# Graph network of four layers on one core: in the second sweep, PSUM results leave by the scalar engine, row-tile pairs stand closer, score vectors are spread later, and the last row tile is treated like the others

## The chip, the cores and the metric

The kernel runs on one core of a Trainium2 chip. The metric is the device time of one execution in microseconds. The time before the change is 2900.31 us, the median of four runs that lie between 2897.81 and 2901.46. All data are 32-bit floats.

## The reference

Four graph layers follow one another on `x` (2708 x 512) with one dense adjacency matrix `adj` (2708 x 2708). Each is added to its input and normalized by rows. Cut to what matters:

```python
deg = jnp.maximum((adj != 0).astype(jnp.float32).sum(-1), 1.0)
x = _layernorm(x + _L0_gnn_ref(x, adj))           # adjacency with normalized mask, divided by its row sums
x = _layernorm(x + _L1_gnn_ref(x, adj, adj, ...)) # below
x = _layernorm(x + _L2_gnn_ref(x, adj, weight))   # x@w0 + adj@x@w1 + adj@adj@x@w2 + ...
x = _layernorm(x + _L3_gnn_ref(x, adj, deg, W, b))# relu((dinv*(adj+I)*dinv @ x + x) @ W + b)

def _L1_gnn_ref(x, adj_a, adj_b, W_sa, a_sa, W_gcnb, b_gcnb, Wa, ba, Wb, bb):
    attn_a = sigmoid(concatenate([adj_a @ x, x], 1) @ Wa.T + ba)
    attn_b = sigmoid(concatenate([adj_b @ x, x], 1) @ Wb.T + bb)
    h = x @ W_sa
    scores = (h @ a_sa[0, :Hd])[:, None] + (h @ a_sa[0, Hd:])[None, :]
    e = where(adj_a != 0, exp(-leaky_relu(scores, 0.01)), 0.0)
    x_a = (e / (e.sum(1, keepdims=True) + 1e-05)) @ h
    x_b = adj_b @ (x @ W_gcnb) + b_gcnb
    return sigmoid(attn_a * x_a + attn_b * x_b)
```

## The kernel before

**Sweeps.** The product of the adjacency matrix with a feature matrix is the kernel's work. It is done in seven sweeps over the matrix, and the sweep with index `s` starts at position `S[s] = 28 * s` of a list. A sweep uses a scheme of seven block products in place of eight: the matrix is cut into two by two blocks, VectorE makes sums of blocks of the adjacency (L405), and TensorE multiplies them (L460) with sums of blocks of the features, `B11`, `B21`, `B22`, `T1` to `T4`, whose tiles carry a letter from A to D for the step of 128 rows that they belong to. In the first two sweeps the rows of the result are cut into ranges, `RANGES = [(0, 384), (384, 384), (768, 256), (1024, 330)]` (start, width). Each range takes seven positions of the list; a product goes through ten steps `k`, two matmuls in each, that add up in the PSUM banks `accu`, `accc`, `accd` and `acca`.

**Order.** Every piece of work is put into a list with `at(position, function)`. The list is sorted by position, and the functions then issue their instructions in that order. Each engine runs its own instructions strictly in the order in which they were issued, and waits at the first one that is not ready. So a position in the list decides what stands behind what on every engine. Tiles come from pools with fixed numbers of buffers: a ring of 38 for adjacency tiles, 6 natural-layout tiles (`nat`), and the 8 banks of PSUM. The tile framework adds the semaphores.

**What the second sweep does.** It forms `adj @ x` for the second layer, with `x` the result of the first layer, whose last rows are still being normalized when the sweep starts (L818, then L557 to L569; the bank that L818 reads comes from L591). While the sweep runs, VectorE also counts the nonzero elements of each adjacency tile into `deg` (L966); SyncE loads those tiles (L396), and GpSimd stores their sums to `As` (L408) for later sweeps.

**Pairs of row tiles.** When a range's product is ready, `done1` multiplies it by `W_gcnb`. Two row tiles, one of each half of the rows, are done together with the same scheme of seven products, in `seven`. One bank holds the quarters `u` and `c`, another `d` and `a`, each 256 wide. Part 0 makes three products of two matmuls into `u`, `c` and `d`; part 1 makes four, which go on in `a`, `u`, `c` and `d`. After each part VectorE adds the quarters to the two output tiles `y` (L654), with the bias row `vec` in place of the old value where an output is touched for the first time. After part 1, ScalarE multiplies each tile of `y` by its gate (L1017), and GpSimd stores it to `XB` (L151). The pairs of one range run beside the next range's sweep. They are three, three and two, and the last range has none. The same `seven` serves the last sweep, where a list `scales` is given and line L656 is used in place of L654.

**Score vectors.** `spread_v` spreads four vectors of 512 numbers, held as columns in `vmat`, over all 128 partitions: sixteen transposes (L891) into four `pv` banks, and eight copies by ScalarE (L894) into tiles that the scheme has free. The function `score` multiplies row tiles by them on VectorE (L903). A row transposition into `ps_r` (L924) follows where the scores of a set of tiles are done.

**The last row tile.** At the end of the kernel the six last row tiles of the output are multiplied by the weights one by one. For the first five, function `b` makes a full-width product by `dense` (L608), one VectorE operation that scales and adds the bias (L1547), then `finish` with ReLU and sum (L1483), the layer norm with its last step on ScalarE (L567), and the store. For the sixth (83 rows) `b_last` does it in halves of 256 columns and divides the last step between ScalarE and VectorE.

Of the kernel before, what the change touches and what calls it, by code (L numbers as in the profile page):

```python
# [21 lines left out]
F32 = mybir.dt.float32  # L22
BF = mybir.dt.bfloat16
AF = mybir.ActivationFunctionType
ALU = mybir.AluOpType
P = 128
EPS = 1e-5
NH = 1354
# [40 lines left out]
def gnn_kernel(ctx: ExitStack, tc: tile.TileContext, x, adjT, w_sa, a_sa, w_gcn, b_gcn, wab, bab, w_hop, w_out,  # L69
               b_out, out):  # L70
    nc = tc.nc
    N, D = x.shape
    NT = 2 * KT
    DC = D // P
    HD = D // 2
# [5 lines left out]
    small = ctx.enter_context(tc.tile_pool(name="small", bufs=6))  # L81
# [9 lines left out]
    neg_half = const.tile([P, 1], F32, name="neg_half")  # L91
# [18 lines left out]
    rdeg_f = const.tile([P, 24], F32, name="rdeg_f")  # L110
# [36 lines left out]
    def move(queue, dst, src):  # L147

        m = dst.shape[0]
        c = m - m % 16 if m > 16 else m  # L150
        queue.dma_start(out=dst[:c], in_=src[:c])  # L151
        if c < m:
            queue.dma_start(out=dst[c:m], in_=src[c:m])
# [7 lines left out]
    def trans(nm):  # L161
        return pool.tile([P, 384], F32, name=nm, tag="ring", bufs=RING)
# [7 lines left out]
    def bank(nm, shape=None):  # L170
        return psum.tile(shape or [P, D], F32, name=nm, tag="x", bufs=8)
# [6 lines left out]
    def at(pos, fn, hold=False):  # L178

        def go():  # L180
            n = len(nc.cur_bb.bb.instructions)
            fn()
            held.update(range(n, len(nc.cur_bb.bb.instructions)))

        events.append((pos, len(events), go if hold else fn))
# [454 lines left out]
    def seven(part, Y, wop, H, lo, w, outs, scales, bases):  # L640

        if part == 0:
            x, y = bank("ps_7"), bank("ps_7")
            H.update(u=x[:, :HD], c=x[:, HD:], d=y[:, :HD], a=y[:, HD:])
        for home, a, v in SEV[part]:
            for c in range(2):
                nc.tensor.matmul(H[home][:w], Y[a, c][:, lo : lo + w], wop(v, c),  # L647
                                 start=part == 0 and home in "ud" and c == 0, stop=c == 1, skip_group_check=True)

        def acc(i, e, home, first=False):  # L650
            o = outs[i][:w, e * HD : (e + 1) * HD]
            b = bases[i][:w, e * HD : (e + 1) * HD] if first else o
            if scales is None:
                nc.vector.tensor_tensor(o, H[home][:w], b, ALU.add)  # L654
            else:
                nc.vector.scalar_tensor_tensor(o, H[home][:w], scales[i], b, ALU.mult, ALU.add)  # L656

        if part == 0:
            acc(0, 0, "u", True)
            acc(1, 1, "c", True)  # L660
            acc(1, 1, "d")
        else:
            acc(0, 0, "a")
            for i, e in ((1, 1), (0, 1), (1, 0)):
                acc(i, e, "u", (i, e) != (1, 1))
            acc(1, 0, "c")
            acc(0, 1, "d")

    def fetch(src, nm="ld"):
        t = nat(nm)  # L670
        move(nc.sync, t[: src.shape[0]], src)
        return t
# [4 lines left out]
    S = [28.0 * s for s in range(8)]  # L677
# [172 lines left out]
    for k in range(KW):  # L850
        f = k / KT
# [13 lines left out]
    W = {}  # L865
    vec = {}
# [26 lines left out]
                V[j, e] = homes[2 * j + e]  # L893
                nc.scalar.copy(V[j, e], ps[:, e * HD : (e + 1) * HD])  # L894

    at(S[1] + 0.5, spread_v)

    def score(t, w, got):
        x1 = got[t]
# [41 lines left out]
    i = 0  # L941
# [55 lines left out]
    def done1(p0, dp, last, R0, n, h, C, tiles):  # L997
        Z = {}

        def gates():  # L1000

            pg = bank("pg")
            for c in range(DC):
                nc.tensor.matmul(pg[32 * c : 32 * c + 32, :n], wab_pad[:, c, :], C[h, c][:, :n], start=True, stop=True)
            Z[0] = trans("zg")
            nc.scalar.copy(Z[0][:, :n], pg[:, :n])

        def gate_tile(i, t, lo, w):
            if i == 0:
                Z[1] = bank("pz", [P, 8])  # L1010
            pz = Z[1][:, 2 * i : 2 * i + 2]
            nc.tensor.matmul(pz[:w], Z[0][:, lo : lo + w], pick, start=i == 0, stop=True, skip_group_check=True)
            nc.vector.tensor_tensor(gate[:w, t, :], pz[:w], gate_x[:w, t, :], ALU.add)
            nc.scalar.activation(gate[:w, t, :], gate[:w, t, :], AF.Sigmoid)

        def finish(t, w, y):
            nc.scalar.mul(y[:w], y[:w], gate[:w, t, 1:2])  # L1017
            move(nc.gpsimd, XB[t], y[:w])

        at(p0 + 0.05, gates)  # L1020
        for i, (t, lo, w) in enumerate(tiles):
            def b(i=i, t=t, lo=lo, w=w):
                gate_tile(i, t, lo, w)
                if not last:
                    return
                px = dense(lambda c: C[h, c][:, lo : lo + w], W[1], w)
                y = nat("y")
                nc.vector.tensor_tensor(y[:w], px[:w], vec[1][:w], ALU.add)
                finish(t, w, y)

            at(p0 + 0.25 + (dp * i if last else 0.02 * i), b)
        if last or h:
            return

        Y = {}
        at(p0 + 0.3, lambda: Y.update(row_sums({(i, c): C[1 - i, c] for i in range(2) for c in range(DC)}, n)))
        for i, (t, lo, w) in enumerate(tiles):
            H, y = {}, []

            def b7(part, t=t, lo=lo, w=w, H=H, y=y):  # L1040
                if part == 0:
                    y.extend(nat("y") for _ in range(2))
                seven(part, Y, W[8], H, lo, w, y, None, [vec[1], vec[1]])
                if part == 1:
                    for j in range(2):
                        finish(t + KT * (1 - j), w, y[j])

            at(p0 + 0.6 + 1.1 * i, lambda f=b7: f(0))
            at(p0 + 0.6 + 1.1 * i + 0.2, lambda f=b7: f(1))

    sweep(S[1], RANGES, extra=extra1, done=done1, late=0.85, save=True)

# [425 lines left out]
    def done6(p0, dp, g, i0, n, h, cc, tiles):  # L1478
# [12 lines left out]
        for i, (s, lo, w) in enumerate(tiles[:3] if not end else ()):  # L1491
            H, got, z = {}, {}, []
            r = 12 * g + 6 * h + lo // P
# [14 lines left out]
            p = p0 + 0.35 + 0.95 * i  # L1508
# [3 lines left out]
        for i, (s, lo, w) in enumerate(tiles[3:] + tiles[:3] if end else ()):  # L1512
            got = {}
            r0 = i0 + s * n + lo

            def a(r0=r0, w=w, got=got):
                got["x"] = fetch2(X3, h, r0, w)

            def b_last(s=s, lo=lo, w=w, r0=r0, got=got):

                r = 12 * g + 6 * h + 3 * s + lo // P
                y = got["x"]
                st = small.tile([P, 2, 6], F32, name="st2", bufs=1)
                for e in range(2):
                    q = slice(e * HD, (e + 1) * HD)
                    px = bank("ps_d")
                    for c in range(DC):
                        nc.tensor.matmul(px[:w, q], cc(s, c)[:, lo : lo + w], W[6][c][:, q], start=c == 0,
                                         stop=c == DC - 1, skip_group_check=True)
                    nc.vector.scalar_tensor_tensor(px[:w, q], px[:w, q], rdeg_f[:w, r : r + 1], vec[6][:w, q], ALU.mult,  # L1530
                                                   ALU.add)
                    nc.vector.scalar_tensor_tensor(y[:w, q], px[:w, q], 0.0, y[:w, q], ALU.max, ALU.add)
                    nc.vector.bn_stats(st[:w, e, :], y[:w, q])
                mv = small.tile([P, 2], F32, name="mv")
                nc.vector.bn_aggr(mv[:w], st[:w])
                rstd = small.tile([P, 2], F32, name="rstd")
                nc.vector.tensor_scalar(rstd[:w, 0:1], mv[:w, 1:2], EPS, None, ALU.add)
                nc.gpsimd.tensor_tensor(rstd[:w, 1:2], rstd[:w, 0:1], neg_half[:w], ALU.pow)
                nc.vector.scalar_tensor_tensor(rstd[:w, 0:1], mv[:w, 0:1], -1.0, rstd[:w, 1:2], ALU.mult, ALU.mult)
                nc.scalar.activation(y[:w, :HD], y[:w, :HD], AF.Identity, bias=rstd[:w, 0:1], scale=rstd[:w, 1:2])  # L1540
                nc.vector.tensor_scalar(y[:w, HD:], y[:w, HD:], mv[:w, 0:1], rstd[:w, 1:2], ALU.subtract, ALU.mult)
                move(nc.sync, out[h * NH + r0 : h * NH + r0 + w, :], y[:w])

            def b(s=s, lo=lo, w=w, r0=r0, got=got):
                px = dense(lambda c: cc(s, c)[:, lo : lo + w], W[6], w)
                r = 12 * g + 6 * h + 3 * s + lo // P
                nc.vector.scalar_tensor_tensor(px[:w], px[:w], rdeg_f[:w, r : r + 1], vec[6][:w], ALU.mult, ALU.add)  # L1547
                finish(s, lo, w, got["x"], px)

            p = p0 - 0.095 + 0.14 * i  # L1550
            at(p - 0.6, a)
            at(p, b if i < 5 else b_last)

    sweep2(S[6], 0, done6, True)

# [8 lines left out]
    for n, i in enumerate(list(nc.cur_bb.bb.instructions)):  # L1564
        p = last if n < 3 * strict else done if n in held else {}
# [44 lines left out]
```

## Time and profile before

| | |
|---|---|
| median of four runs | 2900.31 us (2897.81 to 2901.46) |
| profiled execution, its own time | 2900.08 us |
| span of the profiled execution | 2898.3 us |
| outside the span | 1.78 us |
| mean granted TensorE clock | 0.995 |
| TensorE (PE) busy | 2841.8 us, 98% |
| VectorE (DVE) busy | 2270.5 us, 78% |
| ScalarE (ACT) busy | 563.7 us, 19% |
| GpSimd (POOL) busy | 618.5 us, 21% |

The profile is of one execution. Its engines are PE (TensorE's matmuls), PEld (its weight loads), DVE, ACT, POOL and SP (SyncE); SPq and ACTq stand for those engines' DMA issues. L12 is line 12 of the kernel. A row of the timeline gives the start in microseconds, the duration, the engine, the line, the operation, the tiles written and read, the shapes, and how many instructions are drawn together (x4); in brackets stands how long the engine was idle before it, and what ended that wait. Where instructions of one engine overlap, the distance of their starts is what each costs in a row. One matmul of 32-bit floats appears as two records.

### The profile page before, as it was taken

The page shows a single profiled execution, that of the slowest core. Times are in us where ns is not written, and L with a number is a line of the kernel's source. Part 1 is how long each engine was busy: PE and PEld are TensorE (multiplying, and loading weights), DVE is VectorE, ACT ScalarE, POOL GpSimd, SP SyncE. Part 2 cuts the span into 40 slices and gives each one's busy share as a digit, 9 for nine tenths or more (in the row PEclk, how much of TensorE's full clock was granted, in tenths as well). Part 3 has the DMA queues.
Part 4 walks back from the last instruction along what each step waited for, and adds up shares of the span by engine and source line. Part 5 has one row for each costly group of instructions (what it writes and reads, how often), then busy time and mean ns, then how long its engine had stood idle before and what let it go on. Part 6 is the DMA issues. An engine that isn't in the chain of part 4 may idle for free. (4 is left out here: it accounts for less than half of the span.)

```text
span 2898.3 us, 37726 instructions
## 1 busy us (share of the span) xinstructions
PE 2841.8 (98%) x10963; PEld 1874.5 (65%) x10963; DVE 2270.5 (78%) x5879; ACT 563.7 (19%) x1106; POOL 618.5 (21%) x1119
## 2 busy tenths in 40 slices
PE   7999999999999999999999999999999999999998
PEld 6655665567765666866666666666666666666665
DVE  6989698666647775776699787887878878799987
ACT  4544200101136544552100000000000100100001
POOL 0223223223320111122203123031230211501202
PEclk9999999999999999999999999999999999999999
DMA  7666466444544433565667767566675666754552
GB/s 231 211 192 188 139 199 219 128 155 137 175 148 118 135 119 96 145 197 157 201 195 231 221 186 249 166 199 212 186 249 167 183 196 182 233 163 143 174 142 91
DMA packets 373456, 511.52 MB, mean 176 GB/s; under 512 B 63723, under 2 KB 326629, under 8 KB 373249
## 3 DMA queue, kind: packets, MB, share of 16 engines
q1 hardware_dynamic: 307128, 372.01, 44.4%
q0 software_dynamic: 49536, 126.39, 12.7%
q10 hardware_dynamic: 16584, 10.71, 1.4%
q8 instruction: 87, 1.43, 0.2%
q14 instruction: 121, 0.98, 0.1%
HBM read 425.22 MB, written 83.67 MB: 176 GB/s over the span
## 5 line engine op out<-in xcount | busy, mean ns | idle before, releaser
L1223 DVE TENSOR_TENSOR z<-z 128x339 f32<-128x339 f32 (+1 forms) x966 | 454.0, 502 | 13.2 <-PE accu L1276 3.3
L1294 ACT COPY q<-accu 128x338 f32<-128x338 f32 (+1 forms) x84 | 34.6, 443 | 1005.1 <-PE accu L1276 976.6
L562 POOL TENSOR_TENSOR rstd<-rstd,neg_half 128x1 f32<-128x1 f32 (+3 forms) x91 | 58.4, 642 | 769.6 <-DVE rstd L561 518.8
L1276 PE MATMUL accc<-s,t 128*128 128x338 f32 (+1 forms) x644 | 198.2, 450 | 0.0
L1276 PE MATMUL accu<-z,t 128*128 128x338 f32 (+1 forms) x644 | 194.5, 449 | 2.3 <-DVE z L1223 2.3
L1276 PE MATMUL accc<-z,t 128*128 128x338 f32 (+1 forms) x644 | 194.8, 450 | 0.5 <-ACT q L1294 0.5
L1276 PE MATMUL accd<-z,t 128*128 128x338 f32 (+1 forms) x644 | 193.9, 448 | 0.6 <-DVE q L1358 0.6
L1409 POOL DMA_DIRECT2D Y<-y x192 | 104.8, 552 | 361.8 <-DVE y L1404 332.9
L405 DVE TENSOR_TENSOR a<-a,a 128x384 f32<-128x384 f32 (+2 forms) x330 | 161.8, 510 | 13.2 <-PE accu L460 12.0
L1276 PEld LDWEIGHTS accc<-z,t 128*128 128x128 f32 x644 | 122.9, 191 | 62.3 <-issue 1.8
L1276 PEld LDWEIGHTS accc<-s,t 128*128 128x128 f32 x644 | 121.0, 190 | 64.0 <-issue 7.5
L1276 PEld LDWEIGHTS accu<-z,t 128*128 128x128 f32 x644 | 121.8, 190 | 62.4 <-DVE z L1223 2.9
L1276 PEld LDWEIGHTS accd<-z,t 128*128 128x128 f32 x644 | 122.0, 190 | 60.4 <-DVE q L1358 1.5
L1223 DVE TENSOR_TENSOR s<-z 128x338 f32<-128x338 f32 (+1 forms) x322 | 149.5, 503 | 11.8 <-PE accc L1276 7.4
L1300 DVE TENSOR_TENSOR q<-q,accd 128x338 f32<-128x338 f32 (+1 forms) x112 | 55.9, 499 | 114.4 <-PE accd L1276 114.4
L1075 ACT ACTIVATE e<-row,neg_s 128x384 f32<-128x384 f32 (+5 forms) x176 | 100.4, 570 | 77.1 <-DVE e L1077 22.8
L1076 ACT ACTIVATE f<-row,neg_s 128x384 f32<-128x384 f32 (+5 forms) x176 | 99.9, 568 | 19.7 <-PE accc L460 6.3
L1077 DVE TENSOR_TENSOR e<-e,f 128x384 f32<-128x384 f32 (+5 forms) x176 | 87.1, 506 | 18.3 <-ACT f L1076 17.4
L966 DVE SCALAR_TENSOR_TENSOR deg<-a,deg 128x384 f32<-128x384 f32 (+2 forms) x152 | 74.9, 504 | 29.3 <-DMA a<-in_adjT 28.1
L408 POOL DMA_DIRECT2D As<-a x120 | 64.8, 543 | 92.9 <-DVE a L405 84.9
L1078 DVE SCALAR_TENSOR_TENSOR a<-a,e 128x384 f32<-128x384 f32 (+2 forms) x160 | 79.9, 507 | 5.0 <-DMA a<-in_adjT 3.1
L763 DVE SCALAR_TENSOR_TENSOR s<-a,row 128x384 f32<-128x384 f32 (+2 forms) x152 | 75.1, 506 | 6.0 <-ACT row L748 6.0
(689 smaller groups left out, 5963.0 us busy)
## 6 DMA issues: line engine op xcount, KB each, us to landing
z<-As SPq DMA_DIRECT2D x320, 169.5 KB
z<-As SPq DMA_DIRECT2D x320, 169.0 KB
a<-in_adjT SPq DMA_DIRECT2D x240, 192.0 KB
z<-in_adjT SPq DMA_DIRECT2D x240, 169.5 KB
z<-in_adjT SPq DMA_DIRECT2D x240, 169.0 KB
a<-in_adjT SPq DMA_DIRECT2D x120, 165.0 KB
a<-in_adjT SPq DMA_DIRECT2D x112, 128.0 KB
As<-a POOLq DMA_DIRECT2D x60, 192.0 KB, 3.9
```

The lines of the kernel that those rows point to most:

```text
L405: nc.vector.tensor_tensor(A[r, dst, k][:, :n], A[r, a, k][:, :n], A[r, b, k][:, :n], op)
L408: nc.gpsimd.dma_start(out=SD[m][k * P : (k + 1) * P, R0 : R0 + n], in_=A[r, dst, k][:, :n])
L562: nc.gpsimd.tensor_tensor(rstd[:w, 1:2], rstd[:w, 0:1], neg_half[:w], ALU.pow)
L763: nc.vector.scalar_tensor_tensor(t[:w, :n], a[:w, :n], 0.0, row[R0, h][:w, :n], ALU.is_gt, ALU.mult)
L966: nc.vector.scalar_tensor_tensor(d[:w, :n], a[:w, :n], 0.0, d[:w, :n], ALU.not_equal, ALU.add)
L1075: nc.scalar.activation(e[:w, :n], row[R0, h][0][:w, :n], AF.Exp, bias=neg_s[:w, t : t + 1])
L1076: nc.scalar.activation(f[:w, :n], row[R0, h][1][:w, :n], AF.Exp, bias=neg_s01[:w, t : t + 1])
L1077: nc.vector.tensor_tensor(e[:w, :n], e[:w, :n], f[:w, :n], ALU.min)
L1078: nc.vector.scalar_tensor_tensor(a[:w, :n], a[:w, :n], 0.0, e[:w, :n], ALU.not_equal, ALU.mult)
L1223: nc.vector.tensor_tensor(d[:, :n], Z[x + (k,)][:, :n], Z[y + (k,)][:, :n], op)
L1276: nc.tensor.matmul(B[home][:, :n], stat(v, k), a[:, :n], start=bool(start and k == 0), stop=k == nk - 1, skip_group_check=True)
L1409: nc.gpsimd.dma_start(out=rows[:, :, f * P : (f + 1) * P], in_=o[32 * f : 32 * (f + 1), : m * P].rearrange("p (b d) -> p b d", d=P))
```

## The change

It has four parts. In `seven`, where no `scales` are given (the second sweep), part 0 copies `u` and `c` out of PSUM by ScalarE; only `d` is added by VectorE, and the bias is added from SBUF by two more VectorE operations at the end of part 1. The pairs stand 0.56 of a position apart in place of 1.1, and the second part of each 0.26 after the first in place of 0.2. `spread_v` moves from 0.5 to 0.85 behind the start of the second sweep. `b_last` is gone, and the sixth of the last row tiles goes through `b`.

```diff
@@ seven
-        if part == 0:
+        if part == 0 and scales is None:
+
+            nc.scalar.copy(outs[0][:w, :HD], H["u"][:w])
+            nc.scalar.copy(outs[1][:w, HD:], H["c"][:w])
+            acc(1, 1, "d")
+        elif part == 0:
             acc(0, 0, "u", True)
             acc(1, 1, "c", True)
             acc(1, 1, "d")
@@ seven, end of part 1
             acc(1, 0, "c")
             acc(0, 1, "d")
+            for i in range(2) if scales is None else ():
+                e = slice(i * HD, (i + 1) * HD)
+                nc.vector.tensor_tensor(outs[i][:w, e], outs[i][:w, e], bases[i][:w, e], ALU.add)
@@ spread_v
-    at(S[1] + 0.5, spread_v)
+    at(S[1] + 0.85, spread_v)
@@ done1
-            at(p0 + 0.6 + 1.1 * i, lambda f=b7: f(0))
-            at(p0 + 0.6 + 1.1 * i + 0.2, lambda f=b7: f(1))
+            at(p0 + 0.6 + 0.56 * i, lambda f=b7: f(0))
+            at(p0 + 0.6 + 0.56 * i + 0.26, lambda f=b7: f(1))
@@ done6
-            def b_last(s=s, lo=lo, w=w, r0=r0, got=got):
...
@@ done6
-            at(p, b if i < 5 else b_last)
+            at(p, b)
```

More of the change, by code (lines that the diff above doesn't have):

```diff
@@ L1517, in a @@
                 got["x"] = fetch2(X3, h, r0, w)
-            def b_last(s=s, lo=lo, w=w, r0=r0, got=got):
[L1521 to L1542, printed above, removed]
             def b(s=s, lo=lo, w=w, r0=r0, got=got):
```

## The prediction

> **What bounds the kernel now.** I read the busy shares first, then what TensorE waited for, then the granted clock by stretches, then the timeline around each wait.
>
> The page's busy shares:
>
> ```profile
> PE 2841.8 (98%) x10963; PEld 1874.5 (65%) x10963; DVE 2270.5 (78%) x5879; ACT 563.7 (19%) x1106; POOL 618.5 (21%) x1119
> ```
>
> TensorE is the bound, so an edit pays only by removing TensorE's idle time, matmuls at a lower clock, or work behind the last matmul. The second sweep's waits of TensorE (us in total, times, longest):
>
> ```profile
> PE ps L647 <- DVE y L654: 7.6, 4, 2.4
> PE pv L891 <- DVE ld L818: 2.4, 1, 2.4
> PE ps_n L591 <- DVE P1c L521: 2.4, 1, 2.4
> PE ps_r L924 <- DVE y L654: 0.8, 2, 0.5
> ```
>
> L647 is the matmul of `seven`, L654 its add, L891 the transpose of `spread_v`. The third row is not touched by the change. After 850 us TensorE's waits do not lie in edited code, and few are left, so a saving in the second sweep should reach the end. By windows (the column before last but two is the granted clock):
>
> ```profile
> core 0: us, PE busy (x) PEld busy (x) DVE busy (x) ACT busy (x) POOL busy (x), PEclk, DMA share, GB/s
> 440.00:460.00 20.00, 17.58 (x60) 10.69 (x59) 14.69 (x43) 2.40 (x8) 7.84 (x14) 0.91 0.51 171
> 560.00:580.00 20.00, 19.01 (x67) 12.26 (x65) 17.54 (x61) 2.40 (x4) 8.69 (x17) 1.00 0.74 242
> 580.00:600.00 20.00, 18.96 (x66) 12.99 (x67) 13.16 (x48) 1.48 (x3) 5.36 (x10) 0.91 0.66 210
> 680.00:700.00 20.00, 18.52 (x87) 15.91 (x86) 18.18 (x69) 2.88 (x7) 12.83 (x24) 1.00 0.69 229
> 700.00:720.00 20.00, 18.27 (x87) 15.84 (x86) 15.41 (x65) 1.34 (x2) 2.69 (x5) 1.00 0.50 153
> ```
>
> Where a wait of 2 us or more lies (444, 581, 796 us) the clock is 0.91 or 0.92 over the 20 us; where waits of 1.48 and 1.73 us lie (697, 715 us) it is 1.00. 0.09 of 20 us is 1.8 us lost beside the wait. ACT is nearly idle throughout. One wait in the timeline:
>
> ```profile
> 577.75 1.62 SPq L396 DMA_DIRECT2D a<-in_adjT  x2
> 577.95 0.41 DVE L654 TENSOR_TENSOR y<-ps,vec 128x256 f32<-128x256 f32 x1
> 579.29 0.56 DVE L966 SCALAR_TENSOR_TENSOR deg<-a,deg 128x384 f32<-128x384 f32 x1 [0.93 <-DMA a<-in_adjT]
> 579.76 0.42 DVE L654 TENSOR_TENSOR y<-ps,vec 128x256 f32<-128x256 f32 x1
> 580.56 0.42 DVE L654 TENSOR_TENSOR y<-ps,y 128x256 f32<-128x256 f32 x1
> 581.04 1.48 PE L647 MATMUL ps<-w,W 128*128 128x256 f32 x4 [2.03 <-DVE y L654]
> ```
>
> Part 1 may overwrite `u` and `c` only when part 0's three adds have read them. They stand in DVE's in-order queue among the sweep's other work, here with a `deg` between them that waits for its adjacency load.
>
> **Part 1, copies and closer pairs.** For each of the eight pairs two PSUM adds leave DVE in part 0 and two SBUF adds come back in part 1, so DVE's work is the same (adds start 0.33 us apart at 608.5 to 609.5). ACT gains 16 copies; its copies of 128x256 from PSUM in `spread_v` take 0.37 to 0.43 us, so some 6.5 us on an engine that is 19% busy, hidden while they start on time. What decides is the place of each part in the two queues.
>
> What the waits cost before. First range's pairs (three, amid 384-wide products): 2.03 at 581.04; then twelve records up to 585.42 take 4.38 us where the six products of part 0 take 553.44 to 556.03 = 2.59, so 1.79 more; then 0.52 for `ps_r` at 609.96: 4.34. Second (three, amid 256-wide): 1.48 + 1.73 + 0.31 (697.26, 715.24, 721.00) = 3.52. Third (two, amid 330-wide): 2.37 at 796.12 and again 4.38 against 2.59 up to 800.50: 4.16. In all 12.0 us.
>
> What is late after it. In the changed list three steps of two products stand between a pair's parts, not two (beside 384-wide products 3.9 us for 2.6), and DVE has one add to make there, behind ACT's two copies. I replayed both queues by hand with the rows' durations (0.645 us per product and 0.47 per DVE step at 384, 0.43 and 0.34 at 256).
> - First range. The second pair moves ahead, in between the products of `accc`: part 1 could start at 572.4, and its `d` add is done at 569.3: no wait. The third pair's parts come where the second's were, part 1 after the first stretch of `accd`. TensorE is ready at 584.9; the `d` add stands behind a `deg` whose load can be issued only when TensorE releases the buffer, near 579.7. Two loads before took 4.0 us (567.42 to 571.51) and 5.3 us (573.87 to 579.29) from issue to use, so the add is done between 585.2 and 586.2: 0.3 to 1.3 us of wait. `ps_r` follows soon and shares the bank with the third pair's last adds: another 0.5 to 1.0, in place of 0.52. I take 1.6 of waits left, so 4.34 - 1.6 = 2.7. Ends: 1.2 (waits of 1.3 and 1.8) and 3.5; if one wait passes 2 us the slow stretch returns, and the gain is below 1.
> - Second range. The replay has no wait at the second pair and 0 to 0.6 at the third: 3.52 - 0.3 = 3.2, ends 2.9 and 3.5. DVE was 18.18 of 20 us busy at 680 to 700, and the third pair's nine adds (3.0 us) now come near there; this is the place where the replay is weakest.
> - Third range: part 1 of the second pair at 788.0, its `d` add done at 786.0: all of 4.16 gone. Room is 2 us, so a load 4 us late would bring 2 of it back.
>
> On the other queues: each pair's two `XB` stores (L151, 1.15 us at 803.70) move ahead with it on POOL, which waits in order for the gate multiplies; behind it stand the stores of `As` (L408), which free the sweep's buffers for SP's loads. POOL is 21% busy and has idle stretches of some 2 us around 580, so I take nothing; without that cover a load comes about 1 us later per pair, which is inside the ends above.
>
> Sum of part 1: 2.7 + 3.2 + 4.2 = 10.1 us.
>
> A rule speaks against 3.6 us of that. The Trainium skill, "TensorE: Matmul & The Clock Gate", section on the HAM clock gate, has the array fall to half clock after at least one idle window of about 3.4 us. No wait here is that long, and by the rule the two slow stretches (1.79 each) would have another cause and stay; the estimate by it would be 6.5 for this part. The row decides for me: half speed follows each of the waits of 2.03 us and more and none of those up to 1.73.
>
> **Part 2, `spread_v` later.** The sixteen transposes go behind six more 384-wide products (`B11C`) and ahead of `B11D`. Now they cost a wait of 2.42 and a slow stretch: the four products from 444.82 to 449.09 take 4.27 against 2.58, so 1.69; together 4.1. The rows:
>
> ```profile
> 443.53 0.74 DVE L818 SCALAR_TENSOR_TENSOR ld<-ps_n,rd,ld 128x512 f32<-128x512 f32 x1
> 444.33 0.65 PE L891 MATMUL pv<-ident,vmat 128*128 128x128 f32 x4 [2.42 <-DVE ld L818]
> 447.34 0.41 DVE L569 TENSOR_SCALAR B11D<-ld,mv,rstd 128x256 f32<-128x256 f32 x1
> 449.90 0.41 DVE L569 TENSOR_SCALAR B11D<-ld,mv,rstd 128x256 f32<-128x256 f32 x1 [0.70 <-POOL rstd L562]
> ```
>
> After it the six products run from 440.44 to 444.3 (6 x 0.645), when L818 has freed the bank, and the transposes (12 started in 1.3 us, so 1.8 for 16) end at 446.1. But the next products read `B11D`, which DVE writes at 447.34 and 449.90, after a layer norm that does not depend on this work of TensorE. So a new wait of 1.6 us stands before `B11D`, 1.29 of products follow, another 1.2 us of wait, and the second two products end at 451.6, `accc` starting there and not at 452.96: gain 1.3, not 4.1. If the two waits together lower the clock, the first products hide in the second wait and the second cost 0.85 more: 0.5. I take 1.1. The score operations on DVE that read the vectors start at 457 us, so copies that come 4 us later delay nothing.
>
> **Part 3, the last row tile.** Eight half-width product groups become four of full width: both 3.45 us, TensorE ends at 2890.4 as before. Behind it, before: ACT ends at 2893.83 + 0.60 = 2894.43. After: the full-width chain starts when the previous tile's adds are out of DVE and TensorE ends, 2890.5: L1547 0.75, L1483 0.69, statistics 0.69, aggregate and epsilon 0.31, POOL 0.55 and its hand-over, L564 0.16 and ACT 0.81 (rows of the tile before, 2887.03 to 2887.96 of it on a clear DVE) end near 2894.9. Cost 0.45, ends 0.2 and 1.0. SP's fetch of this tile stays where it was.
>
> **Sum.** 10.1 + 1.1 - 0.45 = 10.7. The profiled execution took 2900.08 (span 2898.3 and 1.78 around it); less 10.7 is 2889.4. The median shown, 2900.31, is 0.2 above the profiled one: 2889.6. The best case is 3.5 + 3.5 + 4.2 + 1.3 - 0.2 = 12.3, and with the 1.5 us by which the four runs lie on either side of the median about 2886.
>
> **Rivals.**
> 1. *The waits move on instead of going* (0.20). The third pair of the first two ranges stands just past 2 us behind DVE: 2.1 + 1.8 each is 7.8, `ps_r` 1.0, and 3.2 is left of 12.0; with 1.1 - 0.45 the gain is 3.9: 2896. For it: the late load in front of the third pair's `d` add, and the 18.18 of 20. Against: one add stands in the way where three did, with half as much room again.
> 2. *Slower: each pair's first results wait for the pair before it* (0.08). ACT's copies of the next pair stand behind two gate multiplies (L1017, 1.33 us), which wait for the last add of the pair before; the `d` add stands behind the same adds on DVE. Room is tightest amid 256-wide products: from the end of a pair's part 1 to the start of the next one's, three steps, a part 0 and three steps, 2.6 + 2.6 + 2.6 = 7.8 us. The chain is eight adds 2.7, then on DVE nine other operations of the list 3.0, and the `d` add 0.33: 6.0 (by ACT 2.7 + 1.33 + 0.75 + 0.33 = 5.1). It decides from 1.8 us of load waits of DVE in that stretch. Past 3.8 each of the five later pairs waits 2.2 + 1.8 = 4.0, 20 in all: 2900.1 + 20 - 12.0 - 1.1 + 0.45, about 2907. For it: DVE waited 0.93 us for a load before 579.29 and some 1.4 before 571.51. Against: that is near the edge once, not past it five times.
> 3. *The change does almost nothing* (0.02): the removed waits are taken up at the next late layer norm or load, 2899 to 2901.
>
> **How the numbers follow.** Less than 0.2% (5.8 us) is about what a measurement of this kernel can't tell from no change. Forecast 0.70 (gains of 6 to 13, all faster); rival 1 lies mostly within 0.2%, as does rival 3; rival 2 is slower. So 0.70, 0.21, 0.09. The range goes from 2886 to rival 1, with 1 us for its spread: 2897.5; left out is rival 2 and the edges.
>
> **What would show it.** Right: TensorE's waits at L647 fall from 7.6 to under 2 us, the windows at 580 and 780 us show a clock of 1.00, ACT shows 16 copies of 128x256 more; the wait at L891 is replaced by waits at L460 for `B11D`, 2.8 us together; the span behind the last matmul is 0.2 to 1.0 longer. Wrong: a new wait at L647 for ACT's copy (rival 2), or waits over 2 us at L647 or L924 with a clock of 0.91 beside them (rival 1); a wait of `accu` on layer norm above 3 us would void part 2.

## The result, and the profile after

The changed kernel takes 2894.91 us in the median of 35 runs, against 2901.35 us in 54 runs of the kernel before on the same chips. The ratio is 0.998, with a 95% interval from 0.9975 to 0.9985. So it is faster by some 5.8 us (4.4 to 7.3). The forecast was 10.7 us. The direction was right and the time lies in the range, but only about half of the gain came. The profiled execution has a span of 2892.6 us against 2898.3.

The page's busy shares, of after:

```profile
PE 2836.6 (98%) x10955; PEld 1869.1 (65%) x10955; DVE 2268.8 (78%) x5875; ACT 568.9 (20%) x1122; POOL 618.4 (21%) x1119
```

ACT has the 16 copies more, at a cost of 5.2 us of its busy time. What TensorE's matmuls waited for from 433 to 850 us, of after (us in total, times, longest; lines behind the edit have moved down by eight):

```profile
PE accu L460 <- DVE B11D L569: 3.8, 2, 2.8
PE pg L1012 <- DVE C L521: 2.4, 1, 2.4
PE ps_r L932 <- DVE y L654: 2.1, 1, 2.1
PE ps_r L932 <- DVE rdeg L994: 0.9, 1, 0.9
PE ps L647 <- DVE y L654: 0.6, 1, 0.6
```

The waits at L647 fell from 7.6 to 0.6 us, as forecast, and the wait at `pv` is gone. In their place stand four others, all for VectorE. The first, for `B11D`, was forecast at 2.8 us in all; the third was forecast at 0.5 to 1.0. The second and fourth were not forecast. The windows of after (the granted clock is the last column but two):

```profile
440.00:460.00 20.00, 16.07 (x59) 9.61 (x59) 16.24 (x51) 3.04 (x10) 7.84 (x14) 1.00 0.54 178
...
580.00:600.00 20.00, 17.87 (x63) 11.63 (x62) 16.44 (x68) 3.19 (x7) 7.32 (x14) 0.91 0.96 321
...
780.00:800.00 20.00, 20.00 (x79) 14.68 (x78) 15.98 (x39) 2.64 (x6) 10.26 (x20) 1.00 1.00 325
```

The last of them is what the change was forecast to do: TensorE busy for the whole window, at full clock. The middle one still has 0.91. The rows for it, from the timeline of after:

```profile
582.17 0.42 DVE L654 TENSOR_TENSOR y<-ps,y 128x256 f32<-128x256 f32 x1
...
583.34 1.03 PE L647 MATMUL ps<-w,W 128*128 128x256 f32 x4
...
584.66 0.56 DVE L974 SCALAR_TENSOR_TENSOR deg<-a,deg 128x384 f32<-128x384 f32 x1 [1.94 <-DMA a<-in_adjT]
...
589.23 0.40 DVE L654 TENSOR_TENSOR y<-ps,y 128x256 f32<-128x256 f32 x1
...
590.56 0.73 DVE L654 TENSOR_TENSOR y<-ps,y 128x256 f32<-128x256 f32 x2
591.02 0.27 PE L932 MATMUL ps_r<-ident,rcol 128*6 128x128 f32 x1 [2.13 <-DVE y L654]
...
591.78 4.44 PE L460 MATMUL accd<-a,T1B 128*128 128x384 f32 x8
```

The third pair's `d` add (582.17) is made before TensorE arrives for part 1 (583.34), so there is no wait there. But then VectorE waits 1.94 us for a load and works off sums; the third pair's first add of part 1 starts at 589.23, more than 2 us after TensorE's last product of the pair (it ends near 587.0). The row transposition takes a bank that these adds still read, and waits 2.13 us. The eight records behind it take 4.44 us where 2.74 is usual: a slow stretch.

The new wait near 736 us, of after, and then the place as it was before, by two rows of the same matmuls' weight loads:

```profile
735.29 0.17 DVE L917 TENSOR_TENSOR sc<-sc 128x12 f32<-128x12 f32 x1
...
735.77 0.41 DVE L521 TENSOR_TENSOR C<-U,accc 128x256 f32<-128x256 f32 x1
...
736.24 1.08 PE L1012 MATMUL pg<-C,wab_pad 128*32 128x256 f32 x4 [2.42 <-DVE C L521]
```

```profile
739.42 0.14 PEld L1004 LDWEIGHTS pg<-C,wab_pad 128*32 128x32 f32 x2 [0.33 <-DVE C L521]
...
740.15 0.14 PEld L1004 LDWEIGHTS pg<-W,wab_pad 128*32 128x32 f32 x2 [0.26 <-DVE W L521]
```

Before, VectorE's sums (L521) and TensorE arrived there together: small waits of 0.2 to 0.3 us before the weight loads. The list of the matmuls' waits has no row for them; the list of the weight loads' waits has two, of 0.5 us each in all (`C` and `W`). After, TensorE comes 5.7 us earlier and VectorE only 3.1. In both kernels it makes 24 score operations (the last ends in front of L917) ahead of the sums; experiment 5 shows that they are what holds it. These scores belong to positions 19.15 to 21.05 of the sweep's list and the sums to 19.05 and 19.06. So the description above, that each engine gets the list's order, does not hold for VectorE: the framework lets operations of later positions go first.

**Where the time went.** The table gives, in microseconds, the time between the starts of the same TensorE instructions in the timelines. "Spread" goes from the first `ps_n` (433.21 before) to the `accu` products behind the row transposition near 484; "set 1" from 549.49 to 612.01 before, "set 2" on to 724.56, "gates" (the matmul at L1004 with what stands around it) on to 742.44, "set 3" from 767.64 to 811.38.

| | before | changed | difference | forecast |
|---|---|---|---|---|
| up to the first `ps_n` | 433.21 | 432.35 | -0.9 | 0 |
| spread | 51.24 | 50.56 | -0.7 | -1.1 |
| set 1 | 62.52 | 61.79 | -0.7 | -2.7 |
| set 2 | 112.55 | 109.16 | -3.4 | -3.2 |
| gates | 17.87 | 20.43 | +2.6 | 0 |
| set 3 | 43.74 | 39.42 | -4.3 | -4.2 |
| 1210 to 1571 us | 360.75 | 362.53 | +1.8 | 0 |
| last tile and the rest | | | about 0 | +0.45 |

The first row and the 1.8 us are in code that the change does not touch. Over all kernels run here the stretch from 1210 to 1571 took 359.5 to 362.5, in no order that follows the edits, so I take both for scatter between executions. The stretches from "spread" to "set 3" give 6.5 us less, the last tile 0.3 more (experiment 7): 6.2, which the ratio's 4.4 to 7.3 holds.

Each column is one execution, and a slow stretch that came or did not come is in it. With the same code there, set 1 of the changed kernel took 61.64 in experiment 1 and 59.82 in experiment 7, where the wait at `ps_r` was 1.86 us and no slow stretch followed. The gates took 22.54 in experiment 1, where a slow stretch followed a wait of 2.84. Set 3 with the old pairs took 43.74 before and 42.36 in experiment 9, where a wait of 2.67 us had no slow stretch behind it. So a difference of 2 us in one row can be this alone.

### The profile page after: what moved, and what is told of

Read it like the earlier page. It is cut to its first block, busy times and chain, and to the rows that moved or that the text cites. A ratio compares the mean times of both kernels' runs of the same rounds, so it can differ in the third digit from the quotient of the medians.

```text
span 2892.6 us, 37709 instructions
## 1 busy us (share of the span) xinstructions
PE 2836.6 (98%) x10955; PEld 1869.1 (65%) x10955; DVE 2268.8 (78%) x5875; ACT 568.9 (20%) x1122; POOL 618.4 (21%) x1119
```

## The experiments

All are compared with runs of the kernel before on the same chip. "Set 1" and so on are the stretches of the table.

**1. Score vectors spread early again.**

```diff
-    at(S[1] + 0.85, spread_v)
+    at(S[1] + 0.5, spread_v)
```

> The changed kernel with the score vectors spread at 0.5 of a position again, the rest as changed. Theory A (a saving of TensorE lasts only as long as no VectorE or load chain is as late as TensorE: the profile after shows 1.3 us of gain up to the first accc and 0.66 of it given back at the row transposition near 482 us): slower than the changed kernel by 0.7 us, 0 to 1.3, and the wait at pv is back with 2 us or more. Theory B (the gain of the spread is what it removes, 2.42 of wait and 1.69 of half clock): slower by 3 to 4 us.

Ratio 0.9983 (0.9974 to 0.9991), 2895.68 us: no difference from the changed kernel that can be measured. The wait at `pv` is back with 2.81 us. The spread stretch took 52.20 against 50.56. Theory B does not fit: the stretch is 1.6 us longer, not 3 to 4. In time alone a loss of 4 us would have shown, one of 3 us not.

**2. Old spacing, copies kept.**

```diff
-            at(p0 + 0.6 + 0.56 * i, lambda f=b7: f(0))
-            at(p0 + 0.6 + 0.56 * i + 0.26, lambda f=b7: f(1))
+            at(p0 + 0.6 + 1.1 * i, lambda f=b7: f(0))
+            at(p0 + 0.6 + 1.1 * i + 0.2, lambda f=b7: f(1))
```

> The changed kernel with the pairs 1.1 apart and the second parts 0.2 behind the first again, copies by ScalarE kept. Theory A (place in VectorE's queue decides): most of the waits at L647 are back, 4 us or more in the profile, and the time is slower than the changed kernel by 2 to 5 us. Theory B (ScalarE's copies alone end the waits): waits at L647 under 2 us, time within 1 us of the changed kernel.

Ratio 0.9992 (0.9983 to 1.0001), 2899.81 us: nearly all the gain is gone. The waits of this kernel in the same stretch:

```profile
PE ps L647 <- DVE y L654: 3.6, 2, 2.0
PE ps_r L932 <- DVE y L654: 3.0, 3, 1.8
PE ps_r L932 <- DVE rcol L927: 2.4, 1, 2.4
```

The copies halve the waits at L647 (7.6 before), but row transpositions then wait. Set 2 took 115.24 us, set 3 took 41.31. Theory A holds; the waits at L647 alone are a little under the 4 us it asked for.

**3. Adds on VectorE, new spacing kept.**

```diff
-        if part == 0 and scales is None:
-            nc.scalar.copy(outs[0][:w, :HD], H["u"][:w])
-            nc.scalar.copy(outs[1][:w, HD:], H["c"][:w])
-            acc(1, 1, "d")
-        elif part == 0:
+        if part == 0:
...
-            for i in range(2) if scales is None else ():
-                e = slice(i * HD, (i + 1) * HD)
-                nc.vector.tensor_tensor(outs[i][:w, e], outs[i][:w, e], bases[i][:w, e], ALU.add)
```

> The changed kernel with both PSUM adds of part 0 on VectorE again (bias in them, no copies, no bias adds at the end), the new spacing kept. Theory A (the spacing does the work, a third step between the parts and other neighbours in the queue): within 1.5 us of the changed kernel, waits at L647 under 2 us. Theory B (the copies are needed): waits at L647 of 3 us or more and 2 to 5 us slower.

Ratio 0.9983 (0.9974 to 0.9991), 2896.72 us. In time theory A looks right. But the profile has one wait of 3.90 us at L647 at 590.54 us, with a clock of 0.83 in the window around it, and set 1 took 64.83 against 61.79; the stretches of set 2 (108.99) and set 3 (39.42) were as in the changed kernel. So neither theory as put: the spacing alone does it for sets 2 and 3, and in set 1 the copies are needed (experiment 10 repeats this without what follows behind). Part of that loss is paid back behind it, by a gates stretch of 19.59 for 20.43: a TensorE that comes later waits less there.

**4. The row transposition later.** (`i == 9` is that of the second range's first half of rows.)

```diff
-            at(S[1] + 1.6 + 0.95 * (i - 1), lambda R0=R0, h=h, ts=tiles_of(R0, n): score_rows(R0, h, ts))
+            at(S[1] + (2.1 if i == 9 else 1.6) + 0.95 * (i - 1), lambda R0=R0, h=h, ts=tiles_of(R0, n): score_rows(R0, h, ts))
```

> The changed kernel with one row transposition (that of the scores of the second range's first set of tiles, into ps_r) half a position later, so that it no longer asks for the third pair's bank while VectorE still adds. The profile after shows 2.13 us of wait there and a slow stretch of 1.8 behind it. Theory A: the wait goes, and TensorE is 2 to 4 us earlier at 600 us; but the sums before the gates' matmul near 736 us stand on VectorE behind 24 score operations, and 1 to 3 us of it are given back there: faster than the changed kernel by 1 to 2.5 us. Theory B (no later bound): faster by 3.5 to 4 us. Theory C (all given back): 0.

Ratio 0.997 (0.996 to 0.9981), 2893.11 us, or some 3 us below the changed kernel's ratio. Set 1 takes 57.72 for 61.79: 4.1 us, of which the wait of 2.13 and the 1.7 of the slow stretch are 3.8. The window of 580 to 600 us of this kernel, as above:

```profile
580.00:600.00 20.00, 20.00 (x78) 13.85 (x77) 15.58 (x52) 4.53 (x9) 8.95 (x17) 1.00 0.93 309
```

At the gates it waited 2.0 us, less than the changed kernel's 2.4, so nothing more was given back there than already was. The result lies between A and B; the ratio's interval cannot part them.

**5. The same, and the last three tiles' scores held to their place.** The third argument of `at` keeps an operation behind what its engine was given earlier in the list.

```diff
-                at(S[1] + 1.1 + 0.95 * i, lambda t=h * KT + k, w=wt(k): score(t, w, got1))
+                at(S[1] + 1.1 + 0.95 * i, lambda t=h * KT + k, w=wt(k): score(t, w, got1), i >= 19)
```

> The changed kernel with the row transposition half a position later, as in the run before this, and the score operations of the last three row tiles held to their place in the list, behind the four sums that the gates' matmul near 736 us reads; until now VectorE made all 24 of them ahead of the sums. Theory A (VectorE's queue is what gives the saving back there): the wait at pg of 2.0 us goes, the stretch from the end of the second set of pairs to the matmuls behind pg is back at 17.9 us from 20.0, and the time is 1 to 2 us below the kernel with the transposition alone, 4 to 6 us below the changed kernel. Theory B (the held scores, 24 operations or 10 us, come where the third set of pairs needs VectorE): the wait at pg goes and 2 us or more of waits appear before 810 us: no faster than the transposition alone.

Ratio 0.9953 (0.994 to 0.9967), 2887.14 us. From its timeline:

```profile
729.87 0.75 DVE L521 TENSOR_TENSOR C<-U,accc 128x256 f32<-128x256 f32 x2 [6.99 <-PE accu L484]
...
730.54 0.74 DVE L521 TENSOR_TENSOR W<-W,accu 128x256 f32<-128x256 f32 x2
...
731.21 0.41 DVE L911 SCALAR_TENSOR_TENSOR vy<-ld,B11B 128x256 f32<-128x256 f32 x1
```

VectorE now waits 6.99 us for TensorE, and makes the sums first. The gates stretch takes 16.76 us, 3.7 less than in the changed kernel and 1.1 less than before. Set 3 stays at 39.42: the held scores disturb nothing, and theory A holds. The step in time from experiment 4 is larger than the stretch's 3.3 us, but the two intervals overlap, so the rest is not shown. Of before, then, 1.1 us of this stretch were already VectorE's.

**6. The same, with `b_last` back.** (The function as it was before, and `at(p, b if i < 5 else b_last)`.)

> As the run before, and the last of the last row tiles in halves by b_last again, so three of the four parts of the change and two new places. Theory A: the end behind the last matmul is 0.2 to 0.6 us shorter than in the changed kernel, and the time is within 1 us of the run before. Rival: the end is the same, b_last bought nothing.

Ratio 0.9949 (0.9937 to 0.9962), 2884.87 us. This is the fastest kernel, 14.8 us (11.0 to 18.3) below the kernel before and faster than both. Its advantage of 2.3 us in the median over the run before is more than the tail explains, and within the intervals.

**7. `b_last` alone back in the changed kernel.**

> The changed kernel with b_last alone put back. Read in the profile only: the time from the start of the last tile's matmuls to the end of the span. Theory A: 0.2 to 0.6 us shorter than in the changed kernel (the predicted cost of the removal is 0.45, 0.2 to 1.0). Rival: no difference, or longer.

One run, of 2889.93 us, so there is no verdict in time. Measured in the profiles from the start of the fifth tile's last ScalarE operation (L567) to the end of the span: before 2887.15 to 2898.3, 11.15 us; changed 2881.22 to 2892.6, 11.38; this kernel 2877.02 to 2888.2, 11.18; with the three moves of experiment 6, 11.14. Over all twelve profiles it is 11.4 us without `b_last` and 11.1 to 11.2 with it: removing it costs some 0.3 us. To the end of the last ScalarE operation it is 0.49 (7.77 for 7.28); from there to the end of the span the kernels without `b_last` take 0.2 less, and why is not shown.

**8. The fastest kernel with the early spread.** The edit is that of experiment 1.

> The fastest kernel so far (copies, closer pairs, row transposition later, scores held, last tile in halves) with the score vectors spread at 0.5 again. Theory A (what the spread gains stays where no VectorE bound follows, and the layer norm's chain leaves 1 to 1.5 us of it): from the first transposition of the sweep to the products behind the row transposition near 484 us it takes 51 to 52 us, against 49.1 to 50.6 with the late spread, and the time is 1.4 us longer, 0.5 to 2.5. Rival: no difference.

Ratio 0.9955 (0.9943 to 0.9968), 2885.46 us, 0.6 above the fastest kernel and not told apart from it. The spread stretch took 51.30 against 49.14. Over all profiles this stretch took 49.3 to 52.2 with the early place (four kernels, mean 51.0) and 49.1 to 52.0 with the late one (eight, mean 50.2). So the move gains about 0.8 us, less than one execution differs from another.

**9. The two moves without the change.** The edits of experiments 4 and 5 in the kernel before.

> The kernel before, with only the two moves (row transposition half a position later, last three tiles' scores held in their place). Theory A (the moves pay because the change made TensorE reach those places earlier): 0.5 to 1.5 us faster than before, of which 1.1 by the shorter stretch behind the second pairs (16.8 for 17.9). Rival (the moves are good by themselves): 4 us or more faster than before.

Ratio 0.9995 (0.9986 to 1.0004), 2898.11 us. The gates stretch takes 16.76, as expected, but the waits at L647 are still 7.4 us, and set 2 takes 112.49. Sets 1 and 3 took 60.08 and 42.36, less than before's 62.52 and 43.74, as no slow stretch followed their waits; this profile is that of the shortest of the eleven runs (2893.40). Theory A: the moves pay because the change brought TensorE there earlier.

**10. The fastest kernel with the adds on VectorE.** The edit is that of experiment 3.

> The fastest kernel so far with both PSUM adds of part 0 on VectorE again, no copies and no late bias adds. Theory A (copies matter at one pair only, the third of the first set, where VectorE's adds stand behind a deg that waits for its load): a wait of 3 to 4 us at L647 near 590 us, none elsewhere, the first set's stretch at 62 to 65 us against 57.7, and 4 to 7 us slower than the fastest kernel. Rival (copies are worth little, as the run with adds on VectorE had about the changed kernel's time): within 1.5 us of the fastest.

Ratio 0.9966 (0.9954 to 0.9979), 2890.31 us, 5.4 above the fastest kernel, though the intervals of the two ratios still overlap. Set 1 takes 61.92 against 57.72; sets 2 and 3 are the same. The wait at L647 is where theory A asks for it, but 1.87 us long, not 3 to 4; one of 0.3 us stands at 702.61. From its timeline:

```profile
584.82 0.42 DVE L654 TENSOR_TENSOR y<-ps,vec 128x256 f32<-128x256 f32 x1
...
586.59 0.56 DVE L966 SCALAR_TENSOR_TENSOR deg<-a,deg 128x384 f32<-128x384 f32 x1 [1.21 <-DMA a<-in_adjT]
...
587.07 0.42 DVE L654 TENSOR_TENSOR y<-ps,vec 128x256 f32<-128x256 f32 x1
...
587.54 0.70 PE L647 MATMUL ps<-T3D,d 128*128 128x256 f32 x2 [1.87 <-DVE y L654]
```

It is the row of before again, one pair later: a `deg` that waits for its load stands between the two first adds. The copies take both adds out of this queue. Their worth in this execution is 4.2 us in set 1, about half of it a slow stretch behind the wait. That it shows in the time only where nothing behind takes it back is likely, but not shown by the intervals; in experiment 3 it could not be told from nothing.

## Why the prediction was half right

**Sets 2 and 3 of the pairs** went as worked out: 3.4 for 3.2, and 4.3 for 4.2 us. The replay of the two queues found the right waits and their ends; at the third pair of set 2 it was 0.55 us, in the forecast's 0 to 0.6. The spacing is what does it there (experiments 2, 3). That set 3 agrees so closely is in part because forecast and table use the same profile before: 1.8 of the 4.3 us is its slow stretch, which experiment 9 did not have.

**Set 1: the term for `ps_r` was mis-sized.** The text put it at 0.5 to 1.0 us. It was 2.13 with a slow stretch behind it, and 0.7 us was left of 2.7. The wait at part 1 of the third pair, forecast at 0.3 to 1.3, did not come: the `d` add stood in front of the late load, not behind it, and what the load delayed were the adds of part 1, which `ps_r` waits for. The text had named the outcome, "if one wait passes 2 us the slow stretch returns, and the gain is below 1". Experiment 4, which takes the wait away, gives back 4.1 us in the stretch.

**The step that failed outright** is "a saving in the second sweep should reach the end". I had looked for waits in edited code and after 850 us, and not at 739 us, in between, where TensorE and VectorE were level. There 2.6 of the 5.7 us by which TensorE came earlier were given back. Experiment 5 shows it: with VectorE's queue put in order the stretch falls by 3.7. A list of the matmuls' waits shows only who is late now. Who is just in time showed here in small waits before weight loads, and in what stood in the other engine's queue.

**The spread** was right in kind: the wait at `pv` (2.42) turned into waits for `B11D` (2.83 + 1.00, forecast 1.6 + 1.2). About 0.8 of 1.1 us is left, and experiments 1 and 8 could not part it from nothing in time. **The last tile**: some 0.3 for 0.45, inside the ends. The sum follows ScalarE's end, which moved by 0.49; 0.2 of it was won back behind.

**The clock.** The sum took for certain that a wait of 2 us or more is followed by a slow stretch and one of 1.73 by none. That is not a rule, as the last section shows. So the two slow stretches of 1.79 us in the waits' cost of 12.0 belonged to the one execution that was profiled: none followed the four waits at L647 of experiment 9. By the share of the last section about half of these 3.6 us was to be expected, an estimate. The Trainium skill, "TensorE: Matmul & The Clock Gate", section on the HAM clock gate, asks for an idle window of some 3.4 us that runs free of the kernel. Its length does not fit the rows: slow stretches follow waits of 1.8 to 2.8 us. That the phase is free would fit them, but no run here tests it.

**The rivals.** The first (the waits move on, 2896) came nearest in time, with one of its two places: `ps_r`, but no wait of 2 us at the third pair in sets 1 and 2. The second (ScalarE's queue holds the copies) did not happen: the waits at L647 were 0.6 us, none for ScalarE.

## What to carry to other kernels

When one engine is busy 98% and waits are taken from it, ask at every later meeting with another engine by how much that one is early; the gain ends where that slack ends, and the list of the matmuls' waits in the old profile does not hold it. Walk the queue of the second engine between the edit and the end for operations that could stand later (here 24 score operations ahead of four urgent sums), and put them in order together with the edit: the change alone gave 5.8 us, the two moves alone 1.4 (4 at most), and both together with the old last tile 14.8. A bank that is asked for by a short side job (one transposition) is worth as much attention as the large matmuls' banks.

## What the runs showed of the hardware

TensorE's drop to half clock after a wait is not set by the wait's length alone. In the twelve kernels' profiles 33 waits of TensorE between 1.8 and 2.9 us were seen from 400 to 850 us of the span; 17 were followed by a slow stretch that cost 1 to 3 us (in two of them only behind a second, shorter wait), 16 were not, and none of eight shorter ones, 1.40 to 1.73, was. In a slow stretch the records of 384-wide products start 0.64 us apart, for 0.32 elsewhere. The same transposition at `ps_n` waited 1.82 us in experiment 1 with a slow stretch and 1.82 in experiment 4 without one; in the changed kernel the 2.83 us before `B11D` had none and the window's clock is 1.00. As an estimate from these rows such a wait costs its length and about half of 1.7 us.
